# Selective scans in one list of pieces beside all other work, products shared with GpSimd, and u stored turned

## The chip, the cores and the metric

One core of one Trainium2 chip. The metric is the device time in microseconds (us) of one execution. The kernel before took 9687.55 us (median of 3 runs, 9681.52 to 9706.05). SBUF and PSUM are the two memories beside the engines in which a kernel places its tiles. The granted clock is the share of TensorE's full clock that the profile shows.

## The reference, cut to what matters

Four images of 64 x 64 x 96 pass through layer 0 (a block of in-projection, binary 3x3 convolution, four selective scans, layer norm, gate, out-projection) and layer 1 (attention without softmax, and a feed-forward with 8-bit factors). The scans carry the weight:

```python
delta = jax.nn.softplus(delta + delta_bias[None, :, :, None])
def step(h, inp):
    ut, dt, Bt, Ct = inp
    dA = jnp.exp(dt[..., None] * A[None])
    h = dA * h + (dt * ut)[..., None] * Bt[:, :, None, :]
    y = jnp.einsum('bkdn,bkn->bkd', h, Ct)
    return (h, y)
```

There are 4 images, K = 4 directions (rows, columns, and both backwards), 192 channels, 16 states and 4096 steps: 192 x 16 x 4 x 4 recurrences of 4096 steps, or 1536 pieces of 128 partitions x 1024 steps.

## The kernel before

It takes the images in pairs. For a pair, everything up to the scans' inputs is computed, then all scans, then layer norm and out-projection; layer 1 comes at the end. A piece is 128 channels of one state. B and C of a step are the same for all channels, so TensorE copies each row to 128 partitions by a matmul (`spread`), and it sums over states by adding into PSUM with an identity as weights:

```python
for n in range(NS):                                   # 16 states
    bp = spread("bp", n)                              # PSUM, 128 x 1024
    cp = spread("cp", NS + n)
    nc.scalar.activation(dA, delta[:, cols], AF.Exp, scale=c["an"][:, KIND[T], k, n : n + 1])
    nc.vector.tensor_tensor(dB, du, bp, ALU.mult)     # first product
    nc.vector.tensor_tensor_scan(h, dA, dB, carry, ALU.mult, ALU.add)
    nc.gpsimd.tensor_copy(carry[:, n : n + 1], h[:, CH - 1 : CH])
    nc.vector.tensor_tensor(dB, h, cp, ALU.mult)      # second product
    for j in range(2):
        nc.tensor.matmul(y[:, 512 * j : 512 * j + 512], ident, dB[:, 512 * j : 512 * j + 512], ...)
```

## Time and profile before

| stretch of the span (9661.7 us) | length, us | VectorE busy | GpSimd busy |
|---|---|---|---|
| to the first scan | 665 | 159 | 14 |
| scans of the first pair | 3808 | 3705 | 203 |
| between the pairs | 807 | 275 | 11 |
| scans of the second pair | 3807 | 3705 | 203 |
| after the last scan | 575 | 423 | 95 |

In the two scan stages VectorE is busy 97% of the time and GpSimd 5%. The lines of the profile stand in the prediction.

### The profile page before, as it was taken

The page shows a single profiled execution, that of the slowest core. Times are in us where ns is not written, and L with a number is a line of the kernel's source. Part 1 is how long each engine was busy: PE and PEld are TensorE (multiplying, and loading weights), DVE is VectorE, ACT ScalarE, POOL GpSimd, SP SyncE. Part 2 cuts the span into 40 slices and gives each one's busy share as a digit, 9 for nine tenths or more (in the row PEclk, how much of TensorE's full clock was granted, in tenths as well). Part 3 has the DMA queues.
Part 4 walks back from the last instruction along what each step waited for, and adds up shares of the span by engine and source line. Part 5 has one row for each costly group of instructions (what it writes and reads, how often), then busy time and mean ns, then how long its engine had stood idle before and what let it go on. Part 6 is the DMA issues. An engine that isn't in the chain of part 4 may idle for free.

```text
span 9661.7 us, 55915 instructions
## 1 busy us (share of the span) xinstructions
PE 6867.1 (71%) x20931; PEld 2540.6 (26%) x20931; DVE 8266.2 (86%) x6014; ACT 3015.5 (31%) x2906; POOL 526.9 (5%) x1266
## 2 busy tenths in 40 slices
PE   8976666666676776767897666666666677676766
PEld 2232222222222222222324222222222222222244
DVE  2159999999999999998314999999999999999967
ACT  3143333333333333322314333333333333332223
POOL 0000000000000000000000000000000000000012
PEclk6589999999888989999558999998999899999976
DMA  1000000000000000000100000000000000000011
GB/s 39 7 7 3 3 3 4 3 3 3 3 3 3 4 5 5 5 5 15 29 9 7 3 3 3 3 3 3 3 3 3 3 4 5 5 6 7 12 43 27
DMA packets 110605, 73.14 MB, mean 8 GB/s; under 512 B 95076, under 2 KB 95774, under 8 KB 110238
## 3 DMA queue, kind: packets, MB, share of 16 engines
q1 hardware_dynamic: 110334, 69.58, 2.9%
q8 instruction: 164, 2.69, 0.1%
q14 instruction: 107, 0.88, 0.0%
HBM read 24.71 MB, written 13.37 MB: 4 GB/s over the span
## 4 chain that ended last, share of the span: by engine, by line
DVE 58%; PE 22%; issue 16%; ACT 2%; DMA 1%; SPq 0%; POOL 0%; DVEq 0%; POOLq 0%; ACTq 0%
DVE h L490 32%; DVE dB L488 16%; PE yp L497 8%; DVE dB L495 5%; PE cvps L297 3%; PE cvps L300 3%; DVE y L510 1%; PE bp L474 1%; DVE sd L541 1%; PE mu L522 1%; PE tp L350 1%; PE bc L359 1%; PE dt L364 1%; ACT xr L353 1%; PE at L674 0%
## 5 line engine op out<-in xcount | busy, mean ns | idle before, releaser
L497 PE MATMUL yp<-dB,ident 128*128 128x512 f32 x6144 | 3511.3, 700 | 1404.9 <-DVE dB L495 1401.3
L486 ACT ACTIVATE dA<-delta,al 128x1024 f32<-128x1024 f32 x1536 | 1762.8, 1148 | 4794.9 <-DVE h L490 4752.9
L490 DVE TENSOR_TENSOR_SCAN h<-dA,carry,dB 128x1024 f32<-128x1024 f32 x1152 | 2702.0, 2345 | 37.0 <-DVE dB L488 1.9
L497 PEld LDWEIGHTS yp<-dB,ident 128*128 128x128 f32 x6144 | 1170.5, 211 | 3055.9 <-DVE dB L495 1866.4
L488 DVE TENSOR_TENSOR dB<-du,bp 128x1024 f32<-128x1024 f32 x1536 | 1845.5, 1202 | 140.1 <-PE bp L474 139.2
L495 DVE TENSOR_TENSOR dB<-h,cp 128x1024 f32<-128x1024 f32 x1536 | 1862.0, 1212 | 13.3 <-PE cp L474 3.9
L474 PE MATMUL bp<-rb,selw 99*128 99x512 bf16 (+1 forms) x4096 | 1021.2, 412 | 908.9 <-DVE dB L488 885.0
L474 PEld LDWEIGHTS <-selw 99*128 99x128 bf16 (+1 forms) x8192 | 638.7, 109 | 2683.7 <-issue 2493.2
L474 PE MATMUL cp<-rb,selw 99*128 99x512 bf16 (+1 forms) x4096 | 997.3, 404 | 28.3 <-DVE dB L488 16.5
L490 DVE TENSOR_TENSOR_SCAN h<-dA,dB 128x1024 f32<-128x1024 f32 x384 | 876.9, 2284 | 11.0
L494 POOL COPY carry<-h 128x1 f32<-128x1 f32 x1152 | 406.1, 353 | 8208.9 <-DVE h L490 8208.7
L312 DVE TENSOR_SCALAR t<-t,pv 128x512 f32<-128x512 f32 x48 | 23.3, 486 | 610.5 <-ACT t L308 610.5
L297 PE MATMUL cvps<-tp,cw 128*128 128x512 bf16 (+1 forms) x576 | 358.1, 622 | 2.5 <-ACT u L276 2.5
L300 PE MATMUL cvps<-tp,cw 64*128 64x512 bf16 (+1 forms) x576 | 356.4, 619 | 0.0
L427 ACT ACTIVATE sp<-dps,dbias,pv 128x1024 f32<-128x1024 f32 x96 | 115.5, 1203 | 486.3 <-PE dps L414 285.6
L355 DVE COPY xr<-tp 64x1536 bf16<-64x1536 bf16 x64 | 60.8, 950 | 232.0 <-PE tp L350 232.0
L431 DVE TENSOR_TENSOR delta<-sp,sr 128x1024 f32<-128x1024 f32 x96 | 183.3, 1909 | 46.5 <-ACT sp L430 46.5
L308 ACT ACTIVATE t<-cvps,cbias,csc 128x512 f32<-128x512 f32 x48 | 37.3, 777 | 443.4 <-PE cvps L300 443.4
L350 PE MATMUL tp<-identb,xg 128*64 128x128 bf16 x1536 | 157.5, 259 | 15.1 <-DMA xg<-sg 13.2
L541 DVE RECIPROCAL sd<-sd 128x512 f32<-128x512 f32 x48 | 158.6, 3332 | 10.6 <-ACT sd L540 8.4
L522 PE MATMUL mu<-y,lnm 128*128 128x512 f32 x224 | 130.0, 721 | 45.7 <-DVE yc L532 44.6
L350 PEld LDWEIGHTS <-xg 128*64 128x64 bf16 x1536 | 138.3, 160 | 70.9 <-issue 70.9
(181 smaller groups left out, 3702.9 us busy)
## 6 DMA issues: line engine op xcount, KB each, us to landing
rb<-ibc SPq DMA_DIRECT2D x384, 64.0 KB
xt<-in_x SPq DMA_DIRECT2D x16, 384.0 KB
xr<-in_x SPq DMA_DIRECT2D x32, 192.0 KB
x1d<-o SPq DMA_DIRECT2D x32, 192.0 KB
x<-x1d SPq DMA_DIRECT2D x16, 384.0 KB
out<-o SPq DMA_DIRECT2D x32, 192.0 KB
xg<-sg SPq DMA_DIRECT2D x16, 172.0 KB
cwf<-in_cw_t SPq DMA_DIRECT2D x2, 864.0 KB
```

Source lines behind the costliest of these rows:

```text
L297: nc.tensor.matmul(ps[prow, :], c["cw0"][:, t, co], tpad[j][:, win[0], win[1]], start=(t == 0), stop=False)
L300: nc.tensor.matmul(ps[prow, :], c["cw1"][rows, t, co], tpad[2][rows, win[0], win[1]], start=False, stop=(t == 8),)
L350: nc.tensor.transpose(tp[:, j // 6, 128 * (j % 6) : 128 * (j % 6) + 128], src, identb)
L474: nc.tensor.matmul(ps[rows, 512 * h : 512 * h + 512], w.to_broadcast([99, rows.stop - rows.start]), t[:, 512 * h : 512 * h + 512], start=True,
L486: nc.scalar.activation(dA, delta[:, cols], AF.Exp, scale=c["an"][:, KIND[T], k, n : n + 1])
L488: nc.vector.tensor_tensor(dB, du, bp, ALU.mult)
L490: nc.vector.tensor_tensor_scan(h, dA, dB, 0.0 if ci == 0 else carry[:, n : n + 1], ALU.mult, ALU.add)
L494: nc.gpsimd.tensor_copy(carry[:, n : n + 1], h[:, CH - 1 : CH])
L495: nc.vector.tensor_tensor(dB, h, cp, ALU.mult)
L497: nc.tensor.matmul(y[:, 512 * j : 512 * j + 512], ident, dB[:, 512 * j : 512 * j + 512], start=(n == 0), stop=(n == NS - 1),)
L522: nc.tensor.matmul(ps, c["lnm"][:, m, :], src[s], start=(i == 0), stop=(i == len(terms[T]) - 1))
L541: nc.vector.reciprocal(sd, sd)
```

## The change

Its intent: keep VectorE's scans going from almost the first to almost the last microsecond, with the rest of the four images put beside them in small steps, and take products off VectorE. The decays dA go to PSUM instead of SBUF. The program is scheduled by hand. A prologue is an image's work before its scans; then come the turn of y (a transposition, columns for rows) and the epilogue; all are generators, advanced a step for each piece of the list. Where loads and waits are told below, "a turn" is one such step. u "turned" is u transposed, as the column scans need it. The two files differ almost everywhere (the diff has 1944 lines); this is the core, with cuts marked.

```diff
-        for pr in range(NB // 2):
-            layer0_pair(tc, a, pr, pairp, locals())
-    layer1(tc, a, x1d, out, ident, eps5, hmask)
+    scans.run(behind)                      # behind = prologues, turns, epilogues, layer 1 as generators
 ...
+    def run(self, back):
+        for i in range(n):                 # 1536 pieces of 32 channels x 4 states
+            self.loads(i)                  # B, C, delta and delta*u, copied over partitions by DMA
+            if i >= 1: self.carry(i - 1)   # ScalarE
+            if i + 1 < n: self.decay(i + 1)        # ScalarE: exp(delta * A), into one of 2 PSUM buffers
+ ...                                       # evacuate or reduce piece i - 3 (TensorE, ScalarE)
+            if i + AHEAD < n: self.inject(i + AHEAD)   # first product, GpSimd
+            self.scan(i)
+            if i % 8 == 1 and self.todo:
+ ...
+                lanes.append(self.prepare())   # delta for a later chunk
+            interleave(lanes)
+            next(back, None)
 ...
+        pool = c.vec.us + 1.2 > c.gps.us + 2.4     # tally of the work given to each so far
+        h = c.p.h.tile(...) if pool else dA
+        c.vec.tensor_tensor_scan(h, dA, w, first, ALU.mult, ALU.add)
+        (c.gps if pool else c.vec).tensor_tensor(w, h, cr, ALU.mult)   # second product
 ...
+        for x in range(4):                 # sum over the 4 states of a piece: 4 column tiles of 32
+            c.nc.tensor.matmul(y[32 * x : 32 * x + 32, g % 2, :], c.sum4, prod[:, 256 * x : 256 * x + 256],
+                start=(q == 0), stop=(q == NQ - 1), tile_position=(0, 32 * x))
 ...
+                            dst, src = ut[:, :, at : at + 8], u.rearrange("p (h w) -> p w h", w=IW)
+                            nc.scalar.copy(dst, src)       # u turned, stored beside u
```

The rows of signs are multiplied by Wl with all 128 rows of the array in use, and signs are held as fp8 or bf16.

## The prediction

> **What bounds the kernel now.** I read the busy table first, then where in the span each engine is busy, then the costliest groups, then a few microseconds of the timeline.
>
> ```profile
> PE 6867.1 (71%) x20931; PEld 2540.6 (26%) x20931; DVE 8266.2 (86%) x6014; ACT 3015.5 (31%) x2906; POOL 526.9 (5%) x1266
> ...
> DVE  2159999999999999998314999999999999999967
> ...
> L497 PE MATMUL yp<-dB,ident 128*128 128x512 f32 x6144 | 3511.3, 700 | 1404.9 <-DVE dB L495 1401.3
> L486 ACT ACTIVATE dA<-delta,al 128x1024 f32<-128x1024 f32 x1536 | 1762.8, 1148 | 4794.9 <-DVE h L490 4752.9
> L490 DVE TENSOR_TENSOR_SCAN h<-dA,carry,dB 128x1024 f32<-128x1024 f32 x1152 | 2702.0, 2345 | 37.0 <-DVE dB L488 1.9
> ...
> L488 DVE TENSOR_TENSOR dB<-du,bp 128x1024 f32<-128x1024 f32 x1536 | 1845.5, 1202 | 140.1 <-PE bp L474 139.2
> L495 DVE TENSOR_TENSOR dB<-h,cp 128x1024 f32<-128x1024 f32 x1536 | 1862.0, 1212 | 13.3 <-PE cp L474 3.9
> ```
>
> VectorE is at 9 tenths or more in two long blocks, with a gap at the start, one in the middle, and a ragged end. ScalarE waited 4753 us for the scans and hardly anything else; VectorE waits for almost nobody in those blocks. GpSimd is idle. The blocks are the two pairs' scan stages: the first scan starts at 665 us and the last of that pair ends near 4473; the second pair runs from 5280 to 9087. So 7615 us hold 1536 pieces (4.96 us each), and VectorE is busy 7410 of them (97%). The other 2046 us (665 at the start, 807 between the pairs, 575 at the end) are projections, convolution, layer norm and layer 1, beside which no scan runs.
>
> ```profile
> 2000.56 2.28 DVE L490 TENSOR_TENSOR_SCAN h<-dA,dB 128x1024 f32<-128x1024 f32 x1
> 2002.76 1.19 DVE L488 TENSOR_TENSOR dB<-du,bp 128x1024 f32<-128x1024 f32 x1
> 2003.87 1.21 DVE L495 TENSOR_TENSOR dB<-h,cp 128x1024 f32<-128x1024 f32 x1
> 2005.00 2.28 DVE L490 TENSOR_TENSOR_SCAN h<-dA,dB 128x1024 f32<-128x1024 f32 x1
> ```
>
> One round takes 4.44 us, less than the 4.68 of its three durations: an instruction that waits for nothing starts some 0.08 us before the one ahead ends. A scan costs 2.20 us so, a product 1.12.
>
> **What the Trainium skill says.** "GPSIMD Engine Reference", section "Performance versus the Vector engine", measures an f32 tensor_tensor of 2048 elements at 4497 ns on GpSimd against 2293 ns on VectorE. Half of the first is 2.25 us for our 1024; the changed kernel's own balance constants give 0.14 + 1024 x 0.00216 = 2.35. The trace of before has no such GpSimd instruction. "SBUF — State Buffer", section "Who interferes with whom", says that a VectorE instruction with at most one SBUF input, outside the two-port modes, does not contend with GpSimd, and that one with two does. The old scan has two (dA and dB); nothing in this trace shows the conflict, as GpSimd was idle. "TensorEngine Tiling", section "Key Properties", says that different tiles of the array can run matmuls in parallel. Here the trace agrees:
>
> ```profile
> L474 PE MATMUL bp<-rb,selw 99*128 99x512 bf16 x2048 | 670.7, 411 | 619.0 <-DVE dB L488 595.1 <-ACT sr L428 23.6
> ...
> L474 PE MATMUL bp<-rb,selw 99*64 99x512 bf16 x2048 | 350.5, 412 | 289.9 <-DVE dB L488 289.9
> ```
>
> Both rows have 2048 matmuls of the same mean length, but those of 64 columns fill 350.5 us, not 670.7: neighbours on the two column halves ran side by side.
>
> **The change, part by part.** *Scan count.* A piece is now 32 channels x 4 states on the partitions instead of 128 channels of one state; 4 images x 4 directions x 4 chunks x 6 x 4 is again 1536 pieces of 128x1024. No scan work is removed.
>
> *VectorE.* The first product (delta u times B) goes to GpSimd altogether, as B is now copied to all channels by DMA rather than by matmul. The second (h times C) is dealt out while the program is built: the instruction order has 905 on VectorE and 631 on GpSimd. Scan and product on VectorE are now neighbours and dependent, so that pair cannot overlap: 2.33 (mean of the 2345 and 2284 ns forms) + 1.12 = 3.45 us. A scan whose product is on GpSimd costs 2.33 - 0.08 = 2.25. Sum: 905 x 3.45 + 631 x 2.25 = 4542 us. Beside it in the list: 378 half-width operations for delta, 144 for the convolutions of three images, about 180 for the epilogues, each about 0.68 us (the 128x512 f32 forms of before take 663 to 752 ns): 477 us. VectorE in the scan stage: 5020 us.
>
> *GpSimd.* 1536 + 631 = 2167 products x 2.35 = 5090 us. The scan reads dA from PSUM and so has one SBUF input; I assume no lock.
>
> *ScalarE.* 1536 decays x 1.148 = 1763; 1152 carry copies of one column, estimated at 0.28 (a 128x6 form took 285 ns) = 320; 189 delta pieces x 5 operations of 0.6 to 0.78 = 640; three images' signs, convolution and projections at about 170 each = 500; turns, epilogues and evacuations about 630. Together about 3850 us, 72% of the stage, but in bursts. The 123 + 115 us of table loads go away, since Abs, Exp, Ln, Relu and Sign are meant to come from one set.
>
> *TensorE.* The 8192 broadcasting bf16 matmuls (2000 us) go. The sum over states is four f32 matmuls of 256 columns on four column tiles. The old pass of 512 columns started every 0.43 us at full clock, so two passes of 256, all four side by side, come to 0.45 to 0.6 us a piece, about 850 us. The rest in the stage, counted by the forms of before, is 2300: about 3200 in all.
>
> *DMA.* 1280 broadcast loads of 512 KB are 640 MB, about 120 GB/s, against 155 GB/s at 55% share in the first 50 us of before, so under half the capacity. u stored turned makes the column scans' loads contiguous; it costs a strided copy and a store in 128-byte runs, both aside.
>
> *Sign products.* The rows of signs times Wl were 768 matmuls of 64 rows (215 us) after 1536 transposes (157 us); now two blocks of 64 are laid on all 128 rows and the turning is done with fp8 or bf16 signs. That is about 370 us of TensorE made smaller, but for three images of four it lies beside the scans, so I count only image 0's part. Layer norm's reciprocals (159 us) are gone too, outside the scans but for the last image.
>
> *Outside the stage.* Only image 0's path to the first projection stays in front: load, transposes and in-projection about 95 us; 288 convolution matmuls at 0.54 us (their spacing in before, at half clock) = 155; projection of two directions 45; delta and first loads 50: 345 us. At the end, the order shows four of eight column blocks of the last image still to be normed (about 75 us, by f32 matmuls), then its last layer over three lanes (about 85 by ScalarE) and a join of 10: 170 us.
>
> *Sum.* GpSimd (5090) and VectorE (5020) are nearly equal, so the stage is near 5.1 ms plus stalls. Each piece needs a decay from ScalarE, whose buffer (two in PSUM) comes free only when the scan two back is through; where ScalarE has over about 1.6 us of other work in a turn, VectorE waits. I put about a quarter of the pieces in that case, with about 0.7 us each: 270 us. 345 + 5090 + 270 + 170 = 5875 of span; the timed median of before is 26 over its span, so 5900 us.
>
> **Rivals.** *The port lock shows after all*: if every scan blocked GpSimd, its 5090 and part of the 5020 would add up, towards 8000 us or more. Against it: one SBUF input. *ScalarE or the order across engines becomes the bound*: the average is 72%, but a late evacuation or carry holds decays; then the stage would be 5.8 ms and the total 6300. *TensorE is not side by side in f32*: 1.72 us a piece at full clock instead of 0.6, 2640 + 2300 = 4940 us at the best clock and more below it, total 6000 to 6500. The bf16 row speaks against it. *DMA late*: small-run stores sit in the same queue as the delta loads; a few us per store, under 100 in all. *Better than thought*: GpSimd overlaps neighbours as VectorE does, at 2.25 us a product = 4880, with few stalls: 5550.
>
> **Range and chances.** The bound is a sum of measured VectorE times, so under 5550 is unlikely; stalls and GpSimd's true cost make the upper side wider: 5580 to 6350. Even the worst rival but the lock is far under 9687: faster 0.98, within 2% 0.01, slower 0.01.
>
> **What would show it.** Right: VectorE and GpSimd both 85% or more busy over the whole span; the product groups near 1.21 us on VectorE and 2.3 on GpSimd; scans still about 2.3; first scan near 345 us; idle before scans led by ScalarE's decays. Wrong: scans or GpSimd products clearly longer than those (lock); TensorE over 85% busy; VectorE idle before scans mostly behind GpSimd's products or a DMA.

## The result, and the profile after

The changed kernel takes 5802.95 us (median of 4 runs, 5794.66 to 5812.12) against 9696.8 for the kernel before in the same rounds. A ratio is the mean time of one kernel's runs over that of the other's of the same rounds, so it is not quite the ratio of these medians: 0.5984, 95% interval 0.5972 to 0.5997. The prediction of 5900 us (5580 to 6350) held.

From the page of the kernel after: busy times, two rows of the 40 slices, and the costliest groups (line, engine, operation, tiles, shapes, count, then busy us and mean ns of one, then the idle time before them and who ended it). All VectorE and GpSimd work of the list shares a helper's line, L386, so the tiles tell the groups apart.

```profile
span 5810.3 us, 61984 instructions
PE 3439.0 (59%) x19877; PEld 1357.2 (23%) x19877; DVE 5123.3 (88%) x3326; ACT 3711.7 (64%) x5692; POOL 5081.3 (87%) x2291
...
DVE  2199999999889999998998999999999999999961
...
POOL 2199999999889999998998999999999999999950
...
L386 POOL TENSOR_TENSOR w<-dl,bc 128x1024 f32<-128x1024 f32 x1536 | 3578.7, 2355 | 145.2 <-PE yp L1235 65.8
L1194 ACT ACTIVATE dA<-dl,anm 128x1024 f32<-128x1024 f32 x1536 | 1714.0, 1116 | 496.5 <-DVE w L386 259.6
L1235 PE MATMUL yp<-w,sum 128*32 128x256 f32 x12288 | 1318.6, 546 | 853.7 <-ACT ys L1247 450.6
L386 DVE TENSOR_TENSOR_SCAN dA<-dA,cy,w 128x1024 f32<-128x1024 f32 x680 | 1593.1, 2343 | 106.6 <-ACT dA L1194 93.9
L386 POOL TENSOR_TENSOR w<-h,bc 128x1024 f32<-128x1024 f32 x631 | 1484.0, 2352 | 194.9 <-DVE h L386 184.0
L386 DVE TENSOR_TENSOR w<-dA,bc 128x1024 f32<-128x1024 f32 x905 | 1108.5, 1225 | 57.8 <-DVE dA L386 0.9
```

The reader sees two engines full side by side where there was one; scans and VectorE's products as long as before (2343 and 1225 ns against 2345 and 1212); and GpSimd's product at 2355 ns. The row of L1235 shows tiles of the array side by side: the durations of its 12288 passes of 546 ns sum to 6709 us, but the group was busy 1318.6. The sum alone would not prove it, since passes that follow each other on one tile overlap too (6144 x 700 = 4301 us of durations in 3511 busy before); but in the trace the four column tiles start within some 20 ns of each other, and the next four mostly 0.2 or 0.4 us later.

The first scan starts at 274.9 us, the last ends at 5598.8. The view from there to 5599.4, which is taken as the stage, gives, by engine, the busy us and the number of instructions, then the granted TensorE clock, the DMA engines' busy share and GB/s:

```profile
274.90:5599.40 5324.50, 3144.24 (x18742) 1201.72 (x18741) 5026.75 (x3152) 3455.41 (x5310) 5024.48 (x2178) 0.67 0.62 194
```

The columns after the length are TensorE, its weight loads, VectorE, ScalarE and GpSimd. VectorE and GpSimd differ by 2 us, and each is idle about 298 us of the stage.

| | before | predicted | after |
|---|---|---|---|
| before the first scan, us | 665 | 345 | 275 |
| scan stage(s), us | 7615 | 5360 | 5324 |
| VectorE busy in it, us | 7410 | 5020 | 5027 |
| GpSimd busy in it, us | 406 | 5090 | 5024 |
| other time, us | 1382 | 170 | 211 |

### The profile page after: what moved, and what is told of

It is laid out like the page before. It is cut to its first block, busy times and chain, and to the rows that moved or that the text cites. A ratio compares the mean times of both kernels' runs of the same rounds, so it can differ in the third digit from the quotient of the medians.

```text
span 5810.3 us, 61984 instructions
## 1 busy us (share of the span) xinstructions
PE 3439.0 (59%) x19877; PEld 1357.2 (23%) x19877; DVE 5123.3 (88%) x3326; ACT 3711.7 (64%) x5692; POOL 5081.3 (87%) x2291
## 3 DMA queue, kind: packets, MB, share of 16 engines
q1 hardware_dynamic: 575636, 1065.88, 58.8%
## 5 line engine op out<-in xcount | busy, mean ns | idle before, releaser
L386 POOL TENSOR_TENSOR w<-dl,bc 128x1024 f32<-128x1024 f32 x1536 | 3578.7, 2355 | 145.2 <-PE yp L1235 65.8
L1194 ACT ACTIVATE dA<-dl,anm 128x1024 f32<-128x1024 f32 x1536 | 1714.0, 1116 | 496.5 <-DVE w L386 259.6
L1235 PE MATMUL yp<-w,sum 128*32 128x256 f32 x12288 | 1318.6, 546 | 853.7 <-ACT ys L1247 450.6
L386 DVE TENSOR_TENSOR_SCAN dA<-dA,cy,w 128x1024 f32<-128x1024 f32 x680 | 1593.1, 2343 | 106.6 <-ACT dA L1194 93.9
L386 POOL TENSOR_TENSOR w<-h,bc 128x1024 f32<-128x1024 f32 x631 | 1484.0, 2352 | 194.9 <-DVE h L386 184.0
L386 DVE TENSOR_TENSOR w<-dA,bc 128x1024 f32<-128x1024 f32 x905 | 1108.5, 1225 | 57.8 <-DVE dA L386 0.9
L386 DVE TENSOR_TENSOR_SCAN h<-dA,cy,w 128x1024 f32<-128x1024 f32 x472 | 1103.8, 2340 | 11.3 <-ACT dA L1194 10.5
L1235 PEld LDWEIGHTS yp<-w,sum 128*32 128x32 f32 x12288 | 363.7, 137 | 1950.8 <-issue 850.8
L386 DVE TENSOR_TENSOR_SCAN dA<-dA,w 128x1024 f32<-128x1024 f32 x225 | 513.6, 2283 | 41.4 <-ACT dA L1194 32.9
L562 PE MATMUL cv<-tp,cw 96*96 96x512 fp8e5 x1152 | 379.9, 488 | 117.6 <-ACT r L608 89.5
L386 DVE TENSOR_TENSOR_SCAN h<-dA,w 128x1024 f32<-128x1024 f32 x159 | 362.3, 2279 | 32.6 <-POOL w L386 24.5
L386 DVE TENSOR_TENSOR u<-cz,e 96x512 f32<-96x512 f32 x64 | 43.8, 684 | 115.9 <-ACT e L586 108.9
L386 DVE TENSOR_TENSOR pd<-dps,pu 128x512 f32<-128x512 f32 x189 | 130.7, 691 | 8.2 <-DMA pu<-ud 1.8
```

The source lines that it names most:

```text
L386: return getattr(self.eng, name)(out, *args, **kw)
L562: nc.tensor.matmul(ps, c.cw[:, j, t, 96 * h : 96 * h + 96], tpad[j][:, 8 * q + dy : 8 * q + dy + 8, dx : dx + IW], start=(j == 0 and t == ...
L1194: c.nc.scalar.activation(t, self.dlt[i // NQ][0], AF.Exp, scale=c.anm[:, g, NQ * KORD[e] + q : NQ * KORD[e] + q + 1])
L1235: c.nc.tensor.matmul(y[32 * x : 32 * x + 32, g % 2, :], c.sum4, prod[:, 256 * x : 256 * x + 256], start=(q == 0), stop=(q == NQ - 1), tile ...
```

## The experiments

Twelve more runs were made, one of them of the changed kernel again; all were correct. The changed kernel is the base of each. No run puts the first product back on VectorE, or takes the new forms of the convolution, the sign products and the layer norm out again: what these are worth alone was not measured.

### What the side work costs: nothing beside the list

`e7_apart` runs all prologues before the list and all turns, epilogues and last layers after it.

```diff
-    while (0, 1) not in c.ready:
+    while lanes:
         interleave(lanes)
 ...
+    for b in range(1, NB):
+        for _ in prologue(c, b):
+            c.later.tick()
 ...
+    scans.run(iter(()))
 ...
```

> The same one list of scan pieces, but nothing beside it: all four prologues before the list, all turns, epilogues and last layers after it. Theory that the side work is hidden beside the scans almost for nothing: the stage gets shorter only by its VectorE share (to about 4872 balanced, plus some 150 of stalls, so 5000 us), and some 810 us of prologues, 40 of the rest of the first and 2100 of epilogues come to lie outside, about 8200 us in all. Rival, that the side work costs the scans about as much as it takes alone (by stalls): the whole stays under 6600 us.

Measured: 7818.34 us (2 runs). The list runs from 1104.6 to 6069.9 us, a stage of 4965 us; 1105 lie before it and 1748 after it.

```profile
1104.60:6069.90 4965.30, 1657.76 (x13776) 554.66 (x13776) 4870.39 (x2879) 2538.28 (x3822) 4874.63 (x2105) 0.55 0.53 175
```

So putting the side work beside the list takes 1105 + 1748 - 275 - 211 = 2367 us out of the ends and makes the stage 5324 - 4965 = 359 us longer. Of these, 5027 - 4870 = 157 are VectorE's own work (the rebalanced sum had been expected at 4872), and the other 202 are idle time: VectorE is idle 95 us in this stage against 298, and in it waits for no decay at all: the waits for ScalarE's decays that are taken up below all come with the side work. The theory stands; the side work outside was less than expected (2853 us in all against some 3200, the 8200 less the stage of 5000), and the overlap is worth 2008 us.

### What the shares of the two engines do: all second products on VectorE

```diff
-        pool = c.vec.us + 1.2 > c.gps.us + 2.4
+        pool = False
```

> All 1536 second products on VectorE, none on GpSimd. Theory that the stage is the busier of the two engines plus about 290 us of stalls: VectorE 1536 x 3.45 + 471 = 5770 us, GpSimd 1536 x 2.31 = 3548; stage 5900 to 6060, whole 6400 to 6570 us. Rival, that the ScalarE and its waits set the pace and not the two engines' sums: the stage hardly grows and the whole stays under 6100 us.

Measured: 6430.76 us (2 runs), in the range; the stage is 5944 us with VectorE busy 5788 and GpSimd 3584. The stage is again the fuller engine plus a remainder, here 156 us instead of 298. Its waits for decays are fewer (33 us against 145); that this comes from the longer turns, which give ScalarE more time, is likely but was not tested. Sharing the second products is worth 628 us.

### What the place of dA does: two SBUF inputs

The scan reads the decays from PSUM. Were this only for room, SBUF would do. To fit them in, two other pools are cut, and a control has the cuts alone.

```diff
-        w=pool("wp", 9), y=pool("yp", 2), ...
+        w=pool("wp", 8), y=pool("yp", 1), ...          # both runs
-        t = c.p.dA.tile([128, CH], F32, name=f"dA_{i}", tag="dA")      # PSUM
+        t = c.p.dS.tile([128, CH], F32, name=f"dA_{i}", tag="dS")      # SBUF, e1_da_sbuf only
```

> Control for the next run: the changed kernel with 8 instead of 9 buffers for w and 1 instead of 2 for the sums' copies, which frees 6 KB per partition. If those buffers are slack, as I think, within 1% of the changed kernel, 5803 us; if they are needed, GpSimd waits for TensorE to free w and it is some per cent slower.

> The decays dA are written to SBUF instead of PSUM, so every scan (dA, w) and most VectorE products (dA, C) have two SBUF inputs. Theory of the shared port (the skill's): a VectorE instruction and a GpSimd product then shut each other out, so that nearly all of 5013 + 5003 us is serial: the stage goes from 5300 towards 9000 to 10000 us, and the listed durations of GpSimd products (2.35 us) or of scans (2.34 us) rise by about the other's length. Rival: there is no lock for these instructions, the durations stay within 3%, and the time stays within 2% of the control.

Measured: 5830.09 us for the control (within its 1%) and 9531.73 us for dA in SBUF (2 runs each). The groups of the latter, with the same instructions as above:

```profile
L386 DVE TENSOR_TENSOR w<-dA,bc 128x1024 f32<-128x1024 f32 x905 | 2826.6, 3123 | 65.7 <-DVE dA L386 0.9 <-issue 0.5 <-PE xa L636 0.5
L386 DVE TENSOR_TENSOR_SCAN dA<-dA,cy,w 128x1024 f32<-128x1024 f32 x680 | 2495.5, 3670 | 75.2 <-ACT dA L1194 63.4 <-ACT cy L1225 11.7
...
L386 POOL TENSOR_TENSOR w<-dl,bc 128x1024 f32<-128x1024 f32 x1536 | 5773.0, 3780 | 149.3 <-PE yp L1235 61.5 <-DMA bc<-bcd 59.3 <-issue 20.7
```

VectorE's product grew from 1225 to 3123 ns, its scan from 2343 to 3670, GpSimd's product from 2355 to 3780; operations of VectorE that kept one SBUF input (the 378 of delta) stayed at 680 to 692 ns. The stage is 9056 us, a tenth under the 10050 of both engines' work put end to end. This is what the Trainium skill's "SBUF — State Buffer", section "Who interferes with whom", says, and the durations here include the waiting. They rose by 1.3 to 1.9 us, less than the length of the other's instruction (2.3 us) that the expectation named, so some of the work still ran side by side. Two SBUF inputs alone do not make a scan slow: those of the kernel before had two, with GpSimd nearly idle, and took 2345 ns. The place of dA is nearly the whole gain of the change: with dA in SBUF the changed kernel is within 2% of the kernel before.

The kernel after shows the same thing in passing. In the timeline (start, duration, instruction), a 96x96 product with both inputs in SBUF, the second of these:

```profile
2038.92 0.24 DVE L386 TENSOR_TENSOR vks<-vk,vks 96x96 f32<-96x96 f32 x1
2039.20 7.49 DVE L386 TENSOR_TENSOR m<-vks,hmask 96x96 f32<-96x96 f32 x1
```

The one above it has the same size and one input in PSUM. In the 7.49 us GpSimd ran three products in a row. This instruction comes four times: 7.49, 7.86 and 0.40 us beside the list, and 0.25 us after it, where GpSimd is free. In `e7_apart`, where nothing runs beside it, all four take 0.25 or 0.26.

### What the turned store of u is worth

`e4_unturned` drops the turned copy; column scans load 64- and 32-byte runs of the plain one.

```diff
-        ud = (c.utd if k % 2 else c.ud)[b].rearrange("h p (n l) -> (h p) n l", l=IW)
+        ud = c.ud[b].rearrange("h p (n l) -> (h p) n l", l=IW)
 ...
+            if k % 2:
+                raw = u[:, 0 : 64 * n].rearrange("p (l n) -> p l n", l=IW)
+                for rows, chans, lines in cuts:
+                    nc.sync.dma_start(raw[rows], ud[chans, :, lines])
+                v = raw.rearrange("p l n -> p n l")      # VectorE reads it with a stride
 ...
```

> u is no longer stored turned; the column scans load their chunk of u from the plain copy in runs of 64 and 32 bytes. That removes 48 ScalarE copies of 1.1 us and 98 thousand runs of 128 bytes, and adds 524 thousand short runs. At an estimated 0.04 us a run on each of 16 engines (70 MB of mostly short runs took 2.9% of the span before), one chunk's load takes some 20 us of all DMA engines, and the delta loads behind it in the queue come late for GpSimd. Theory that the turned store is needed: 5900 to 6500 us, with VectorE or GpSimd waiting for DMA by some hundred us. Rival, that the loads are early enough and DMA has room: within 1% of the changed kernel, 5750 to 5860 us.

Measured: 5834.98 us (2 runs, 5830 to 5839), so the theory falls. The lines of the DMA queue, after and in this run (packets, MB, share of 16 engines):

```profile
q1 hardware_dynamic: 575636, 1065.88, 58.8%
```

```profile
q1 hardware_dynamic: 993172, 1053.30, 62.9%
```

417,536 more packets cost 62.9% of 5837.7 less 58.8% of 5810.3, or 255 us of all 16 engines: 9.8 ns a packet on one engine, not the 40 that I had worked out from the old kernel's mix. VectorE waited for these loads 4.0 us in all. The turned store gains at most some 30 us, about 0.5%, and one round of times does not settle even that. The trace shows where they lie, and it is not DMA: the product of delta and u, after and in this run:

```profile
L386 DVE TENSOR_TENSOR pd<-dps,pu 128x512 f32<-128x512 f32 x189 | 130.7, 691 | 8.2 <-DMA pu<-ud 1.8
```

```profile
L386 DVE TENSOR_TENSOR pd<-dps,pu 128x512 f32<-128x512 f32 x189 | 164.5, 871 | 10.3 <-DMA pu<-ud 4.0
```

Of the 189, the 96 of the row scans take under 0.7 us as before, and the 93 of the column scans, which now read u with a stride, 1.0 to 1.15 us. That is 34 us more of VectorE's work, about as much as the time grew.

### Where VectorE's idle time comes from: bursts of ScalarE, or not

`e6_spread` puts delta's Abs and Relu in two turns. To have time, its pieces start a turn earlier, and `e6b_start0` has that alone.

```diff
-            if i % 8 == 1 and self.todo:
+            if i % 8 == 0 and self.todo:            # both
 ...
         nc.scalar.activation(d[:, 0], ps, AF.Abs, scale=sc, bias=bi)
+        yield                                       # e6_spread only
         nc.scalar.activation(t, ps, AF.Relu, scale=sc, bias=bi)
```

> Control for the next run: delta's pieces start one turn earlier (turn 0 of 8 instead of turn 1). Nothing else changes: within 0.5% of 5800 us by every theory.

> As the control, but delta's first two ScalarE operations (Abs and Relu, 1.5 us together) lie in two turns instead of one. The same work, with lower bursts. Theory that VectorE's waits for decays (about 145 us) come from bursts of over 1.6 us in a turn: 40 to 80 us less than the control. Rival, that they come from ScalarE waiting in its order for TensorE or VectorE: no change, within 15 us.

Measured (4 runs each): 5768.66 us for the control and 5783.37 with the spread. The bursts of this place are not the cause: flatter ones did not help. The control itself was 34 us faster than the changed kernel (0.6%; my expectation of under 0.5% missed), only by which turn the work falls in. Which wait it shortened, the traces show. VectorE's waits for the convolution's exponentials in the stage (us in total, times, longest), in the changed kernel and in the control:

```profile
DVE u L386 <- ACT e L586: 44.3, 28, 3.4
```

```profile
DVE u L386 <- ACT e L586: 14.2, 15, 2.0
```

With the spread they are 34.7 us again. The waits for decays hardly moved: 145 us, 157 in the control, 149 with the spread, so 8 us fewer by the spread where 40 to 80 had been expected.

The trace then showed another cause. The longest waits of VectorE in the stage were these moments; the bracket tells how long the engine had been idle and what ended it.

```profile
1560.66 1.01 PE L1132 MATMUL dps<-gT,wdz 128*128 128x64 fp8e5 x8 [14.79 <-DMA gT<-gTd]
...
1561.71 0.78 ACT L1137 ACTIVATE pd<-dps,dbias,pvd 128x512 f32<-128x512 f32 x1 [8.23 <-PE dps L1132]
...
1565.65 1.12 ACT L1194 ACTIVATE dA<-dl,anm 128x1024 f32<-128x1024 f32 x1
...
1566.87 2.36 DVE L386 TENSOR_TENSOR_SCAN dA<-dA,cy,w 128x1024 f32<-128x1024 f32 x1 [8.71 <-ACT dA L1194]
```

Read from the bottom: the scan had waited 8.71 us for its decay. The decay's buffer had been free for some 9 us, but in ScalarE's order it stands behind delta's activation, which had waited 8.23 us for TensorE (and behind a copy, cut here, that waited 2.02 more); and TensorE had waited 14.79 us for a load of signs, issued only in the step that uses it (at 1551.0 us in the timeline). A late load of side work stopped the list through two engines that each take their instructions in order.

`e8_early` issues these loads sooner: a next image's signs three pieces of delta ahead (the recorded text says one), and two or three more turns between load and use elsewhere.

```diff
+            elif (b + 1, KORD[0] % 2) in c.ready:
+                self.load_signs(b + 1, KORD[0])
 ...
             nxt = load(h, 0)                        # turn of y
+            yield
+            yield
+            yield
 ...
                 self.loads(ln, q, ("y0", "y2", "y13", "u", "sz", "xb"))
                 yield
                 yield
+                if not self.alone:
+                    yield
+                    yield
+                    yield
```

(The last layer gets one more turn in the same way.) A run of the changed kernel on the same chip is its control.

> The changed kernel unaltered, as the control of the next three on the same chip: 5795 to 5812 us by every theory.

> The changed kernel with the loads of the side work issued some turns earlier than their matmuls: a next image's delta signs one piece ahead, and two or three more turns between load and use in the turn of y, the sums and the last layer. Theory that the long waits for decays (the eight of 3.5 to 8.7 us make 46 of the 162 us of waits for ScalarE's decays and carries) come from a late DMA, through TensorE and ScalarE that take their instructions in order: 40 to 100 us less than the control, and no wait of VectorE for ScalarE's decays above 4 us. Rival, that such waits come from ScalarE's own load: within 15 us of the control.

Measured (4 runs each): control 5802.35 us (ratio to before 0.5994), early loads 5749.88 (0.5937, interval 0.5927 to 0.5947). In the view of VectorE's waits (us in total, times, longest), after and with early loads:

```profile
DVE dA L386 <- ACT dA L1194: 126.8, 84, 8.7
```

```profile
DVE dA L386 <- ACT dA L1207: 84.9, 71, 2.8
```

The long waits are gone and the time fell by 52 us, within the expected 40 to 100. Against its control, all waits for decays in the stage fell from 148 us to 106, and those for the convolution's exponentials from 46.5 to 31.0. The theory of late loads holds for the long waits; some 106 us of short ones stay, the 84.9 shown and 21.3 before scans that write elsewhere than over dA.

### A shorter softplus, and all of it together

Delta = ln(1 + exp(x)) needs two activations and no addition. It is the same function while exp(x) does not overflow; x is small here, and the result stayed correct.

```diff
-        nc.scalar.activation(d[:, 0], ps, AF.Abs, scale=sc, bias=bi)
-        nc.scalar.activation(t, ps, AF.Relu, scale=sc, bias=bi)
-        yield
-        nc.scalar.activation(d[:, 0], d[:, 0], AF.Exp, scale=-1.0)
+        nc.scalar.activation(d[:, 0], ps, AF.Exp, scale=sc, bias=bi)
+        yield
         nc.scalar.activation(ps, d[:, 0], AF.Ln, bias=1.0)
         yield
-        c.vec.tensor_tensor(ps, ps, t, ALU.add)
```

> Delta's softplus as ln(1 + exp(x)), in two ScalarE operations instead of four and without the addition on VectorE (valid here as x stays small). ScalarE loses 264 us, VectorE 129; the balance then puts 36 more second products on VectorE, so both engines' sums fall by about 85. Theory that the stage is the balanced sum plus stalls from ScalarE's bursts: 85 of sum and 30 to 60 of stalls, 5655 to 5690 us. Rival, that the stalls have nothing to do with ScalarE's load: 85 only, 5715 us; rival that other waits take the place: 5780 to 5810.

Measured: 5694.89 us (4 runs, 5686 to 5709). That is 108 us less than the changed kernel's 5803 and just above the range. The traces say what made it: the stage is 5219 us, with VectorE busy 4926 in it, 101 less than before and more than the 85 expected, and idle 293 against 298. So the part of the stalls that was to bring 30 to 60 us brought 5. ScalarE had 233 us less to do in the stage (3222 against 3455), and yet the waits for decays were 163 us, not under the 145 of the changed kernel; only those for the convolution's exponentials fell, to 19. The rival that the stalls do not hang on ScalarE's load came nearer.

`e9b` joins this with the earlier start; `e9_best` adds the early loads.

> Softplus in two operations and delta's start one turn earlier, together. If the two gains add, as they concern different things (105 us and 30 us): 5650 to 5680 us; if both only moved the same stalls: 5690.

> The former with the early loads as well. Theory of late DMA loads: another 40 to 100 us less than the former, 5570 to 5630 us. Rival (ScalarE's load): as the former within 15 us.

Measured (4 runs each, beside the control above): 5684.12 us for the first, ratio to before 0.5867, and 5630.4 us for the second, 0.5818. The first is above its range: 118 us gained where the two alone gave 108 and 34. They shorten the same waits: those for the convolution's exponentials are 44 us in the stage of the changed kernel, 14 with the earlier start, 19 with the short softplus and 9 with both. Over the short softplus alone (ratio 0.5873) the earlier start adds nothing clear of noise in time. The early loads add their 54 us in full; the total is at the upper end of its range. The best version takes 0.5818 / 0.5994 = 0.971 of the changed kernel's time.

## Why the prediction was right

**The bound.** The step that the stage is the sum of VectorE's or GpSimd's work plus stalls held: 5027 and 5024 us of work against 5020 and 5090, and moving all second products to VectorE moved the stage to that engine's new sum plus 156. GpSimd's term was 66 too high because its neighbours also overlap: three products in a row take 6.97 us in the timeline, 2.32 each, and from one start to the next in a row it is 2.31 on average. The terms of the sum erred in both directions: the front 70 too high, the bound some 65, the end 41 too low, the stalls 28. The 26 us that the prediction added for timed median over span is no fixed cost: a timed run is 1.8 us over its own span (5812.12 against 5810.3), and the 26 lay between the profiled run and the median of others.

**No lock.** The assumption that one SBUF input keeps the scan out of GpSimd's way was the one on which the time hung; the run with dA in SBUF shows it, at 9532 us. The rival's figure for a lock, "8000 us or more", was right too.

**TensorE.** Side by side in f32 as predicted, but a piece takes 1318.6 / 1536 = 0.86 us, not 0.45 to 0.6. The estimate was for full clock, and the granted clock was 0.67 in the stage against 0.91 before; 0.86 x 0.67 = 0.58 is inside the estimate, and in `e7_apart`, at 0.55, a piece takes 0.97. The total came to 3144 us against 3200, since other terms were smaller. It bounds nothing.

**ScalarE.** 3455 us against 3850: a carry copy takes 0.156 or 0.186 us, not 0.28, and a decay 1.116, not 1.148; these two make some 180 of the difference, the rest lies in the rough terms. The table loads went as said (one of 1.3 us is left).

**DMA.** "About 120 GB/s" and "under half the capacity" was wrong: I counted only the broadcast loads. All intermediate stores and reloads together are 1066 MB on the queue, 194 GB/s and 62% in the stage. It had room even so. The worth of the turned u, which the prediction did not price, is within a per cent, and it lies in VectorE's reading and not in DMA.

**Stalls.** 298 us of idle VectorE against 270 was right in size and wrong in make-up; the size was luck. The step "about a quarter of the pieces wait 0.7 us because ScalarE has over 1.6 us of other work in a turn" failed. VectorE waited 99 times, 145 us in all, for decays and 44 us for the convolution's exponentials; the large ones came from late loads, through TensorE and ScalarE; flatter bursts did not help, nor did 233 us less of ScalarE's work in the stage (`e5_softplus2`). The dependent step from a scan to its product leaves about 0.06 us 905 times (57.8 us), which is part of the 298. What made the remaining short waits was not taken apart.

**The ends.** The front was 70 us too long in the sum, in all its terms: the convolution matmuls of image 0 ran from 81.1 to 194.5 us, so the parts before took 81 us against the 95 given, the convolution's 288 matmuls 113 (0.39 apart) against 155, and what follows up to the first scan 80 against 45 + 50. The mis-sized term is above all the spacing of 0.54, taken from the kernel before at a granted clock of 0.50 (100 to 200 us of its span); here the clock was 0.84 in those 113 us, and the matmuls have another form, 96x96 in fp8. The two were not told apart. The end was 41 too short: the last scan ends at 5598.8, and four normed blocks and the last layer took 211 (197 in the repeat of the same kernel, so runs differ by 14 here).

## What to carry to other kernels

When one engine is full, first look for what can leave it for an idle engine, and check that the two do not meet on the shared SBUF port: keep one input of each VectorE instruction in PSUM while GpSimd works. Side work can be hidden beside a full engine at a small part of its length: here 2367 us of it made the stage 359 us longer, 157 by its own instructions on that engine and 202 by waits. Issue every load it needs well before the instruction that uses it, since a wait in one engine's order stops whatever stands behind it; that took 52 us of these waits away. Read a long wait back through the engines until a DMA or a busy engine ends the chain, rather than trust the first name. And when a run is faster than its control, look in its trace for what changed before naming a cause: here both the short softplus and the turned u gained in VectorE's own work, where stalls and DMA had been expected.

## What the Trainium skill lacked or had wrong

- "SBUF — State Buffer", section "Who interferes with whom": right, with a figure to add. At full use of both engines the lock raised a 1.23 us VectorE product to 3.12 us on average, a 2.34 us scan to 3.67 and a 2.36 us GpSimd product to 3.78, and put a stage of 5324 us at 9056, a tenth under the sum of both engines' work. A 96x96 product took 7.49 and 7.86 us beside GpSimd instead of about 0.25.
- "GPSIMD Engine Reference", section "Performance versus the Vector engine": its 4497 ns for 2048 elements fits; half of it, 2.25 us, was an estimate for 1024, which took 2355 ns, and 2.31 us from start to start in a row.
- "DVE: opcode table, instruction layouts, handler registers and perf-mode slots", section "Datapath and trigger behaviour", says that tensor_tensor_scan runs at half throughput. It fits, and gives no time: 2.28 us for 128x1024 f32, 2.34 with a carried start value in a tile, against 1.21 to 1.23 for a product; unchanged with one input and the output in PSUM.
- "TensorEngine Tiling", section "Key Properties": four f32 column tiles of 32 ran side by side, starting within some 20 ns of each other (6709 us of passes in 1318.6 us of busy time); the section has no measured figure.
- "DMA: Bandwidth & Descriptors", section "Bandwidth", puts a packet at about 10.5 ns, from the span of one 4 KB transfer of 64 packets. That is not the time of one packet on one engine, of which the section has no measurement: in this kernel's queue each net packet more, mostly of 64 or 32 bytes, cost 9.8 ns of one engine here. That the two figures lie close is no agreement.
